# A spatially adaptive convolution in two layers: half of image 0's preparation moved from the prologue into the main loop, with x loads, row stores and squares of the prologue rearranged

## The chip, the cores and the metric

One core of a Trainium2 chip runs the whole program. The metric is the device time of one execution in microseconds; a kernel's time is the median of its runs. Engines are called PE (TensorE matmul), DVE (VectorE), ACT (ScalarE), POOL (GpSimd) and SP (SyncE, which here only issues DMAs). Each engine works through its own queue of instructions in order.

## The reference, cut to what matters

The input x has 4 images of 16 channels, 256 x 256 pixels. Two layers follow; each normalises its input by groups of two channels (8 groups per image) and adds its result to it.

```
# layer 0: h = groupnorm(x); 25 logits per channel and pixel from a 3x3 convolution of h
logits  = conv3x3(h, conv_w) + conv_b              # 16 * 25 = 400 channels
weights = softmax(logits over the 25)
x = x + sum over the 25 of weights * (5x5 neighbourhood of h)
# layer 1: a 3x3 convolution of silu(h) and of 8 cubic B-spline bases of h, h = groupnorm(x)
x = x + conv3x3(silu(h), base_w) + conv3x3(bsplines(h), spl_w) + bias
```

## The kernel before, in words

The program has three stages. The prologue (from line 404 on) computes the group statistics of x, all four images, and prepares image 0. layer0 (line 620) is the main loop of layer 0. layer1 (line 886 on) does layer 1. Only the first two are touched.

**What "preparing" an image is.** Layer 0 reads its normalised input h from DRAM in three layouts: hs (rows, cut in strips, with borders of two pixels; it gives the 5x5 neighbourhoods, tile u), hst (columns, f32; it gives the convolution's main operand, tile am) and hsl (columns again, split into a rounded part hi and a remainder lo; it gives tile an). The columns of hst and hsl are kept apart for the upper and the lower 128 rows of the image (half 0 and half 1), each with one row of the other half as its border. normalize (line 264) is a generator that makes them, for four groups of four channels (q) and both halves (h):

- rows(q): for each half, ACT writes the row tile hsp (line 327) and the column-ordered tile ht (line 340), two instructions each; put_rows (line 286) stores hsp to hs.
- columns(q, n, h): PE transposes four blocks of ht into the PSUM tile tp (line 362); tt and hi are copied from it with the border row (lines 355 to 359), hi always by ACT, tt by DVE in the prologue and by ACT in the main loop; DVE computes lo = tp - hi (line 370); border (line 312) copies lo's border rows. put_columns (line 294) stores tt, hi and lo, a DMA each for each half (line 302): 16 calls of columns and 48 such DMAs per image.

A step of the generator ends at each yield. Stores and loads are put into a list, moves, with the number of steps after which they are issued. All of them are on SP's queue.

**The prologue.** x comes in 8 tiles of 128 rows (four images, two halves; line 423). The first two stay in SBUF (held), the others rotate through three buffers (xin, bufs=3). For each tile, DVE takes bn_stats for every group (lines 534 and 536), with two steps of image 0's normalize after each group; then ACT squares the tile (xq, line 543, one instruction) and PE sums the squares over channels (line 546), from which a bound on the logits is made. At the end of each image come group_stats (small operations, line 140 on), and after all of it a flag (line 589) that says whether the softmax may leave out its maximum. SP loads that flag (line 1112), every engine branches on it, and layer0 starts. A tile scheduler, not the program text, fixes the order on each engine in this stage.

**The main loop.** Each image is worked in 16 strips of 128 rows by 32 columns (two halves of 8 strips), each strip in 8 steps of 4 columns: PE makes logits lg from am and an (lines 833, 837), ACT takes the exponential e (line 856), POOL multiplies by the neighbourhood (line 861), DVE sums over the 25 (nd, line 700) one step later. Three DVE operations and a POOL operation finish a strip (lines 720 to 728); every four strips ACT does the statistics for layer 1 (line 748) and stores the result. load_im (line 640) fetches am and an two pairs of steps ahead, load_u (line 667) a strip's u half a strip ahead, all on SP. In every step one step of the next image's normalize is taken (ahead): images 1 to 3 are prepared in the loop of the image before. The order here is pinned to the text. e has 4 buffers, am and an 3, lg 3, tp 1.

Throughout, every DMA issue on SP or ACT also takes one of 8 completion counters in turn and waits until that counter's DMA before it has landed.

Of the kernel before, what the change touches and what calls it, by code (L numbers as in the profile page):

```python
# [34 lines left out]
def conv_preact_kernel(  # L35
# [34 lines left out]
    QC = 4  # L70
# [192 lines left out]

    def normalize(b, ptr, tiles, held=None, copier=None):

# [4 lines left out]

        moves = [(20 + 4 * i, f) for i, f in enumerate(zeros(b, nc.sync))] if held is None else []

        def move():
            for f in [f for i, f in moves if i <= 0]:
                f()
            moves[:] = [(i - 1, f) for i, f in moves if i > 0]

        def load(q, h):
            if held is None and q < C // QC:
                nc.sync.dma_start(  # L280
                    xps[h][:, :, PAD : PAD + W],
                    x[b, q * QC : (q + 1) * QC, h * P : (h + 1) * P, :].rearrange(
                        "c p w -> p c w"),
                )

        def put_rows(q, h, hsp):
            r0 = PAD + h * P
            nc.sync.dma_start(
                hs[b][:, r0 : r0 + P, q * QC : (q + 1) * QC, :].rearrange(
                    "s r c w -> r s (c w)"),  # L290
                hsp.rearrange("p s c w -> p s (c w)"),
            )

        def put_columns(q, n):
            g0 = n * QG
            for h in range(NH):

# [19 lines left out]
        def rows(q):  # L317
            for h in range(NH):
                xp = xps[h] if held is None else held[h][:, q * QC : (q + 1) * QC]
                hsp = prep.tile([P, NST, QC, SP], F32, name=f"hsp{b}_{q}_{h}", tag="hsp")  # L320
                ht = prep.tile([P, QW, W // QW, QC], F32, name=f"ht{b}_{q}_{h}", tag=f"ht{h}")
                hts[q, h] = ht
                for k in range(QC // GC):
                    g = q * (QC // GC) + k
                    kc = slice(k * GC, (k + 1) * GC)
                    how = dict(scale=nrm[b][:, 0, g : g + 1], bias=nrm[b][:, 1, g : g + 1])
                    nc.scalar.activation(
                        hsp[:, :, kc, :].rearrange("p s c w -> p c s w"),
                        bass.AP(
                            tensor=xp.tensor, offset=xp.offset + k * GC * (W + 2 * PAD),  # L330
                            ap=[xp.ap[0], [W + 2 * PAD, GC], [SW, NST], [1, SP]],
                        ),
                        AF.Identity, **how,
                    )
                    if k == QC // GC - 1:
                        nc.scalar.copy(hsp[:, 0, :, 0:PAD], zpad)
                        nc.scalar.copy(hsp[:, NST - 1, :, PAD + SW :], zpad)
                        moves.append((4, partial(put_rows, q, h, hsp)))
                    yield
                    nc.scalar.activation(  # L340
                        ht[:, :, :, kc].rearrange("p g w c -> p c w g"),
                        xp[:, kc, PAD : PAD + W].rearrange("p c (w g) -> p c w g", g=QW),
                        AF.Identity, **how,
                    )
                    if k == QC // GC - 1:
                        moves.append((4, partial(load, q + 1, h)))
                    yield

        def columns(q, n, h):

            tp = ptr.tile([P, QG, P], F32, name=f"tp{b}_{q}_{n}_{h}", tag="tp")

            def copy(t, to):

                to(t[:, h, :, 1 : 1 + P], tp)
                if h == 0:
                    to(t[:, 1, :, 0:1], tp[:, :, P - 1 :])
                else:
                    to(t[:, 0, :, RP - 1 :], tp[:, :, 0:1])

            for k in range(QG):
                nc.tensor.transpose(
                    tp[:, k, :], hts[q, h][:, n * QG + k].rearrange("p w c -> p (w c)"), ident
                )
            yield
            copy(tts[n], copier)
            copy(his[n], nc.scalar.copy)
            yield

            nc.vector.tensor_sub(  # L370
                los[n][:, h, :, 1 : 1 + P], tp, his[n][:, h, :, 1 : 1 + P].bitcast(F32)
            )
            if h == NH - 1:
                moves.append((5, partial(border, los[n])))
                moves.append((9, partial(put_columns, q, n)))
            yield
# [3 lines left out]

        for h in range(NH):
            load(0, h)
        yield
        for _ in rows(0):
            move()
            yield
        for q in range(C // QC):
            ahead = rows(q + 1) if q + 1 < C // QC else iter(())
            for n in range(QW // QG):
                for h in range(NH):  # L390
                    for k, _ in enumerate(columns(q, n, h)):
                        if k % 3 == 2:
                            next(ahead, None)
                        move()
                        yield
# [8 lines left out]
    with tc.tile_pool(name="prep0", bufs=2) as prep, tc.tile_pool(  # L404
        name="pre", bufs=1
    ) as pre, tc.tile_pool(
        name="xin", bufs=3
    ) as xin, tc.tile_pool(name="stat", bufs=2) as stat, tc.tile_pool(
# [33 lines left out]
        for r in (4 * C, 6 * C):  # L442
            nc.sync.dma_start(wnr[r : r + 1, :], conv_b)
        nm = 3 * C
        sw = pre.tile([P, 3, 9, nm], F32, name="sw")
# [50 lines left out]
        def prepare1():  # L496
# [10 lines left out]
            for r in range(RT):  # L507
# [3 lines left out]
                for d in range(3):  # L511
                    p = SROWS.index(r + d) * C
                    nc.sync.dma_start(
                        ws[p : p + C, :, r, :],
                        wb1[d * C : (d + 1) * C].rearrange("p (e o) -> p e o", e=3),
                    )
# [4 lines left out]
        hm = pre.tile([P, B * NH], F32, name="hm")  # L521
        xq = pre.tile([P, C, W], F32R, name="xq")
        idr = pre.tile([P, P], F32R, name="idr")
        nc.scalar.copy(idr, ident)
        ahead = iter(())
        for b in range(B):
            st = stat.tile([P, G, NH * (GC if b == 0 else 1), 6], F32, name=f"st0_{b}", tag=f"st0{min(b, 1)}")
            for hf in range(NH):
                n = b * NH + hf
                t = loaded.pop(0)  # L530
                for g in range(G):
                    if b == 0:
# [8 lines left out]
                    next(ahead, None)  # L541

                nc.scalar.activation(xq, t, AF.Square)
                sq = pstat.tile([P, W], F32, name=f"sq_{n}", tag="sq")
                for c in range(C):
                    nc.tensor.matmul(
                        sq, lhsT=idr, rhs=xq[:, c], start=c == 0, stop=c == C - 1
                    )
                nc.vector.tensor_reduce(hm[:, n : n + 1], sq, AX.X, ALU.max)
                next(ahead, None)  # L550
                if n >= NH and n + 3 < B * NH:
                    loaded.append(load_x(n + 3))
            mean, rstd = group_stats(stat, pstat, st, f"x{b}")
# [19 lines left out]
            if b == 0:  # L573
                ahead = normalize(0, ptr0, tiles, held, nc.vector.tensor_copy)
                next(ahead)
# [44 lines left out]
    def layer0(shift):  # L620
# [4 lines left out]
        with tc.tile_pool(name=f"prep{arm}", bufs=2) as prep, tc.tile_pool(  # L625
# [172 lines left out]
            for n, (b, hf, s) in enumerate(strips):  # L798
                if (hf, s) == (0, 0):
                    for _ in ahead:  # L800
                        pass
                    ahead = normalize(b + 1, ptr, tiles) if b + 1 < B else iter(())
                    if b == B - 1:
# [3 lines left out]
                if last:  # L807
                    for _ in ahead:
                        pass
                u = us.pop(0)  # L810
# [351 lines left out]
```

## Time and profile before

| what | us |
|---|---|
| median of 3 runs | 3069.55 |
| lowest and highest of them | 3064.12, 3075.65 |
| the profiled execution, its own time | 3061.86 |
| its span, first to last instruction | 3059.8 |
| DVE busy in the span | 2959.0 (97%) |
| PE busy | 2802.6 (92%) |
| ACT busy | 2236.6 (73%) |
| POOL busy | 1947.6 (64%) |
| first nd (line 700) starts | 136.9 |
| last nd | 2043.9 |

The three stages show in the span like this: the prologue until about 120 us, layer 0 until about 2064 us, layer 1 until the end. DVE's reductions (512 of them, 1748.0 us together) and POOL's products (512, 1788.4 us) fill layer 0. An idle time in these views is put down to what released the engine; where several things were waited for, it is the last.

### The profile page before, as it was taken

How to read it: one execution, taken by the hardware profiler on the slowest of the kernel's cores; microseconds unless marked ns; L12 is line 12 of the kernel's file. 1: busy time of each engine (PE TensorE's matmuls, PEld its weight loads, DVE VectorE, ACT ScalarE, POOL GpSimd, SP SyncE). 2: the span in 40 equal slices, each digit the busy share in tenths (PEclk: the TensorE clock that was granted, in tenths of full speed). 3: DMA queues.
4: the chain of work that ended last, by engine and by line, in shares of the span. 5: the costliest groups of instructions: out<-in, count | busy, mean ns of one | idle time of the engine just before them, and what ended most of it. 6: DMA issues, size and time to landing. Idle time of an engine off the chain costs nothing.

```text
span 3059.8 us, 39743 instructions
## 1 busy us (share of the span) xinstructions
PE 2802.6 (92%) x14248; PEld 1448.2 (47%) x14248; DVE 2959.0 (97%) x1587; ACT 2236.6 (73%) x2587; POOL 1947.6 (64%) x744
## 2 busy tenths in 40 slices
PE   4499999999999999999999999958999999999998
PEld 3366656656656666666666566632222222222222
DVE  7599999999999999999999999998999999999997
ACT  6466765676766566766646546559999999999996
POOL 4199999999999999999999999980100100000000
PEclk7699999999999999999999999978999999999999
DMA  8988977879878778978767667659999999999994
GB/s 273 290 223 221 258 205 209 222 189 257 234 209 240 196 202 225 248 216 220 212 174 200 164 173 194 161 131 198 201 192 195 198 194 189 198 194 202 190 197 91
DMA packets 350929, 626.29 MB, mean 205 GB/s; under 512 B 41330, under 2 KB 216676, under 8 KB 334852
## 3 DMA queue, kind: packets, MB, share of 16 engines
q1 hardware_dynamic: 318020, 605.29, 81.0%
q10 hardware_dynamic: 30960, 15.73, 1.8%
q0 software_dynamic: 1744, 2.64, 0.3%
q8 instruction: 117, 1.92, 0.3%
q14 instruction: 88, 0.72, 0.1%
HBM read 513.95 MB, written 104.24 MB: 202 GB/s over the span
## 4 chain that ended last, share of the span: by engine, by line
DVE 69%; issue 11%; PE 8%; DMA 3%; ACT 3%; POOL 2%; SPq 1%; DVEq 0%; ACTq 0%; POOLq 0%
DVE nd L700 44%; PE lg L833 6%; DVE ta L168 4%; DVE ta L167 4%; DVE tb L168 4%; DVE tb L167 4%; DVE tb L158 2%; PE lg L837 1%; DVE yo L1020 1%; POOL e L861 1%; DVE r L721 1%; DVE nd L720 1%; DVE lo L370 1%; DMA am<-hst 1%; DVE nd L722 1%
## 5 line engine op out<-in xcount | busy, mean ns | idle before, releaser
L861 POOL TENSOR_TENSOR e<-e,u 128x1600 f32<-128x1600 f32 x512 | 1788.4, 3539 | 49.0 <-ACT e L856 30.9
L833 PE MATMUL lg<-wm,am 128*128 128x400 f32 x4096 | 1734.8, 505 | 83.8 <-ACT e L856 53.0
L700 DVE TENSOR_REDUCE nd<-e 128x128 f32<-128x3200 f32 x512 | 1748.0, 3478 | 29.0 <-POOL e L861 28.9
L837 PE MATMUL lg<-wn,an 97*128 97x400 f32 x2048 | 1344.9, 657 | 17.3 <-DMA an<-hsl 17.3
L856 ACT ACTIVATE e<-lg 128x800 f32<-128x800 f32 x1024 | 818.2, 837 | 708.9 <-DVE nd L700 460.5
L833 PEld LDWEIGHTS lg<-wm,am 128*128 128x128 f32 x4096 | 760.9, 192 | 403.3 <-ACT e L856 98.2
L1037 PE MATMUL yp<-ring,wt 128*32 128x512 f32 x6144 | 745.9, 598 | 87.6 <-DVE ring L169 63.7
L837 PEld LDWEIGHTS lg<-wn,an 97*128 97x128 f32 x2048 | 388.3, 190 | 334.5 <-issue 23.6
L1037 PEld LDWEIGHTS yp<-ring,wt 128*32 128x32 f32 x6144 | 203.7, 109 | 621.7 <-issue 427.7
L954 POOL MEMSET sl<- 16x256 f32 x6 | 1.8, 306 | 402.7 <-ACT ta L163 299.8
L169 DVE SCALAR_TENSOR_TENSOR ring<-ta,ta 128x2048 f32<-128x2048 f32 (+1 forms) x64 | 147.9, 2310 | 2.5
L168 DVE TENSOR_TENSOR ta<-ta,ta 128x2048 f32<-128x2048 f32 (+1 forms) x64 | 147.5, 2305 | 2.8 <-ACT ta L166 2.8
L169 DVE SCALAR_TENSOR_TENSOR ring<-tb,tb 128x2048 f32<-128x2048 f32 x64 | 145.6, 2275 | 2.5
L748 ACT ACTIVATE z<-xc,nrm 128x256 f32<-128x256 f32 x240 | 144.2, 601 | 5.3 <-POOL xc L728 1.2
L168 DVE TENSOR_TENSOR tb<-tb,tb 128x2048 f32<-128x2048 f32 x64 | 145.4, 2271 | 0.0
L1047 PE MATMUL yp<-sl,ws 64*32 64x512 f32 (+1 forms) x1032 | 131.3, 602 | 0.0
L954 POOL MEMSET slc<- 16x256 f32 x2 | 0.6, 307 | 203.1 <-ACT ta L163 203.0
L166 ACT ACTIVATE ta<-ta 128x2048 f32<-128x2048 f32 (+1 forms) x64 | 123.4, 1928 | 2.0
L193 POOL TENSOR_TENSOR d<-d,nrz 128x8 f32<-128x8 f32 x4 | 2.7, 669 | 191.8 <-DVE d L191 191.8
L166 ACT ACTIVATE tb<-tb 128x2048 f32<-128x2048 f32 x64 | 120.6, 1884 | 0.0
L973 ACT ACTIVATE sl<-sl,q 64x2048 f32<-64x2048 f32 x43 | 90.0, 2094 | 1.1
L728 POOL TENSOR_TENSOR xc<-xc,nd 128x512 f32<-128x512 f32 x64 | 82.5, 1289 | 8.2 <-DVE nd L722 8.2
(195 smaller groups left out, 2089.3 us busy)
## 6 DMA issues: line engine op xcount, KB each, us to landing
am<-hst SPq DMA_DIRECT2D x512, 194.6 KB
u<-hs SPq DMA_DIRECT2D x320, 288.0 KB
an<-hsl SPq DMA_DIRECT2D x512, 129.8 KB
xta<-x1s SPq DMA_DIRECT2D x40, 1024.0 KB
xtb<-x1s SPq DMA_DIRECT2D x40, 1024.0 KB
xtc<-x1s SPq DMA_DIRECT2D x40, 1024.0 KB
am<-hst SPq DMA_DIRECT2D x256, 129.8 KB
sl<-x1s SPq DMA_DIRECT2D x166, 128.0 KB
```

Of the source, the lines that this page charges most:

```text
L166: nc.scalar.activation(s1, r1, AF.Square, scale=2.0)
L167: nc.vector.scalar_tensor_tensor(s2, t, 2.0, s2, ALU.subtract, ALU.mult)
L168: nc.vector.tensor_mul(s1, s1, r1)
L169: nc.vector.scalar_tensor_tensor(f, s2, 0.0, s1, ALU.min, ALU.subtract if given else ALU.add)
L700: nc.vector.tensor_reduce(nd[:, :, :, j : j + JG].rearrange("p t c j -> p t j c"), e.rearrange("p t j m c d -> p t j c m d"), AX.XY, ALU.add,)
L748: nc.scalar.activation(z, v, f, scale=nrm[b][:, 0, g : g + 1], bias=nrm[b][:, 1, g : g + 1], accum_out=st1[b][:, t, g, columns_of(n) : col ...
L833: nc.tensor.matmul(lg[:, i, :NL], lhsT=am[:, o : o + P], rhs=wm.rearrange("p m c d -> p (m c d)"), start=True, stop=False,)
L837: nc.tensor.matmul(lg[:, i, :NL], lhsT=an[:, o : o + P], rhs=wn.rearrange("p m c d -> p (m c d)"), start=False, stop=True,)
L856: nc.scalar.activation(ev, lg[:, :, :NL], AF.Exp)
L861: nc.gpsimd.tensor_tensor(e[:, 1].rearrange("p j m c d -> p j (m c) d"), e[:, 0].rearrange("p j m c d -> p j (m c) d"), uv, ALU.mult,)
L1037: nc.tensor.matmul(yp[t * M : (t + 1) * M], lhsT=wt[:, d, e].rearrange("p r o -> p (r o)"), rhs=ring[:, r0 + t * RT + d : r0 + t * RT + d ...
L1047: nc.tensor.matmul(yp[t * M : (t + 1) * M], lhsT=ws[v, e].rearrange("p r o -> p (r o)"), rhs=sl[n % 3][v, t : t + NT + 1 : NT, e : e + W], ...
```

## The change: what it does

Of image 0, the prologue makes columns only for half 0. normalize gets an argument part.

- **part=0**, in the prologue: rows are done as before for both halves, and all transposes too, but from half 1 only one border row is copied; of tt, hi and lo a full tile is made for half 0 alone. The border rows that half 1 will need from half 0 are put aside in new constant tiles (kept). put_columns stores half 0 only: 24 DMAs.
- **part=1** (late), in the main loop during image 0's first strips: x's half 1 is loaded again (4 loads of 512 KB), ht is made again, columns are made for half 1 and stored (24 DMAs). tt is copied by ACT here. It must be through before strip 6, and after it follows the preparation of image 1, as a chain.
- **dense=True** for late and for image 1: columns takes 4 steps instead of 6, transposes, copies and lo within one of them.
- **Loads of x**: xin has 4 buffers instead of 3, and tile 5 is loaded right after the convolution's weights.
- **put_rows** in the prologue is issued on ACT's queue, after 1 step instead of 4.
- **Squares**: xq is made in two halves (two buffers), with the PE sums, and stands ahead of the tile's bn_stats in the program.
- The six small DMAs to ws (line 513) go from SP's to POOL's queue.

```diff
-    def normalize(b, ptr, tiles, held=None, copier=None):
+    NQ = QW // QG
+    kept = [
+        const.tile([P, C // QC * NQ, QG, 1], d, name=f"kept{i}") for i, d in enumerate((F32, F32R, F32R))
+    ]
+    def normalize(b, ptr, tiles, held=None, copier=None, part=None, dense=False):
...
+        moves = moves if held is None and part is None else []
+        parts = range(NH) if part is None else (part,)
+        read = range(NH) if part != 1 else (1,)
...
+        def place(q, h):
+            return xps[h if part is None else q % 2]
...
-            nc.sync.dma_start(
+            (nc.sync if held is None else nc.scalar).dma_start(
                 hs[b][:, r0 : r0 + P, q * QC : (q + 1) * QC, :].rearrange(
...
-            for h in range(NH):
+            for h in parts:
                 for to, ti, t in ((hst, 0, tts[n]), (hsl, 0, his[n]), (hsl, 1, los[n])):
...
-                        moves.append((4, partial(put_rows, q, h, hsp)))
-                    yield
+                            moves.append((4 if held is None else 1, partial(put_rows, q, h, hsp)))
+                        yield
...
-            def copy(t, to):
-                to(t[:, h, :, 1 : 1 + P], tp)
-                if h == 0:
-                    to(t[:, 1, :, 0:1], tp[:, :, P - 1 :])
+            def copy(t, to, keep):
+                if h in parts:
+                    to(t[:, h, :, 1 : 1 + P], tp)
+                if part == 1:
+                    to(t[:, 1, :, 0:1], keep[:, q * NQ + n])
+                elif h == 1:
+                    to(t[:, 0, :, RP - 1 :], tp[:, :, 0:1])
                 else:
-                    to(t[:, 0, :, RP - 1 :], tp[:, :, 0:1])
+                    to(t[:, 1, :, 0:1] if part is None else keep[:, q * NQ + n], tp[:, :, P - 1 :])
...
-            yield
-            copy(tts[n], copier)
-            copy(his[n], nc.scalar.copy)
-            yield
+            if not dense:
+                yield
+            copy(tts[n], copier, kept[0])
+            copy(his[n], nc.scalar.copy, kept[1])
+            if not dense:
+                yield
+            v = slice(1, 1 + P) if h in parts else slice(RP - 1, RP)
+            to = h if h in parts else 0
             nc.vector.tensor_sub(
-                los[n][:, h, :, 1 : 1 + P], tp, his[n][:, h, :, 1 : 1 + P].bitcast(F32)
+                los[n][:, to, :, v], tp[:, :, 0 : v.stop - v.start],
+                his[n][:, to, :, v].bitcast(F32),
             )
+            if part == 0 and h == 0:
+                moves.append((1, partial(
+                    nc.scalar.copy, kept[2][:, q * NQ + n], los[n][:, 0, :, P : P + 1]
+                )))
+            if part == 1:
+                nc.scalar.copy(los[n][:, 1, :, 0:1], kept[2][:, q * NQ + n])
             if h == NH - 1:
-                moves.append((5, partial(border, los[n])))
-                moves.append((9, partial(put_columns, q, n)))
+                if part is None:
+                    moves.append((5, partial(border, los[n])))
+                moves.append((9 if part is None else 4, partial(put_columns, q, n)))
...
-        name="xin", bufs=3
+        name="xin", bufs=4
...
+        loaded.append(load_x(5))
...
-                    nc.sync.dma_start(
+                    nc.gpsimd.dma_start(
                         ws[p : p + C, :, r, :],
...
+                sq = pstat.tile([P, W], F32, name=f"sq_{n}", tag="sq")
+                for i in range(2):
+                    xq = pre.tile([P, C // 2, W], F32R, name=f"xq_{n}_{i}", tag="xq", bufs=2)
+                    nc.scalar.activation(xq, t[:, i * C // 2 : (i + 1) * C // 2], AF.Square)
+                    for c in range(C // 2):
+                        nc.tensor.matmul(
+                            sq, lhsT=idr, rhs=xq[:, c], start=i + c == 0,
+                            stop=(i, c) == (1, C // 2 - 1),
+                        )
                 for g in range(G):
...
-                nc.scalar.activation(xq, t, AF.Square)
-                sq = pstat.tile([P, W], F32, name=f"sq_{n}", tag="sq")
-                for c in range(C):
-                    nc.tensor.matmul(
-                        sq, lhsT=idr, rhs=xq[:, c], start=c == 0, stop=c == C - 1
-                    )
...
-                if n >= NH and n + 3 < B * NH:
-                    loaded.append(load_x(n + 3))
+                if n >= NH and n + 4 < B * NH:
+                    loaded.append(load_x(n + 4))
...
-                ahead = normalize(0, ptr0, tiles, held, nc.vector.tensor_copy)
+                ahead = normalize(0, ptr0, tiles, held, nc.vector.tensor_copy, 0)
...
-                    ahead = normalize(b + 1, ptr, tiles) if b + 1 < B else iter(())
+                    ahead = normalize(b + 1, ptr, tiles, dense=b == 0) if b + 1 < B else iter(())
+                    if b == 0:
+                        late = normalize(0, ptr, tiles, part=1, dense=True)
+                        ahead = chain(late, ahead)
...
+                if n == NST - 2:
+                    for _ in late:
+                        pass
```

## The prediction

> **What bounds the kernel now.** I read the busy time per stretch first, then DVE's and ACT's own timelines around the start of layer 0, then the waits.
>
> Stretches of 20 us (columns: length; busy us and instructions of PE, PE's weight load, DVE, ACT, POOL; granted clock; DMA share; GB/s), and below them a stretch of the main loop from another answer of the same view:
>
> ```profile
> 80.00:100.00 20.00, 11.45 (x52) 10.17 (x53) 14.46 (x31) 16.12 (x23) 0.00 (x0) 0.59 1.05 339
> 100.00:120.00 20.00, 6.13 (x32) 4.78 (x31) 14.63 (x52) 7.14 (x22) 1.84 (x2) 0.59 1.07 359
> 120.00:140.00 20.00, 13.47 (x40) 8.27 (x41) 3.09 (x1) 3.35 (x4) 7.24 (x18) 0.76 1.01 253
> 140.00:160.00 20.00, 12.09 (x35) 7.43 (x34) 10.34 (x4) 9.62 (x13) 9.91 (x4) 0.74 0.78 190
> ...
> 660.00:1170.00 510.00, 484.12 (x1693) 312.02 (x1691) 508.26 (x206) 337.62 (x598) 493.83 (x153) 0.98 0.81 218
> ```
>
> From 660 to 1170 us DVE is busy 508.26 of 510: layer 0 is DVE's. So the change can save only before DVE's dense run begins, and each DVE instruction that it puts into the loop is paid in full. The dense run begins here:
>
> ```profile
> 136.91 6.97 DVE L700 TENSOR_REDUCE nd<-e 128x128 f32<-128x3200 f32 x2 [16.95 <-POOL e L861]
> 153.11 3.49 DVE L700 TENSOR_REDUCE nd<-e 128x128 f32<-128x3200 f32 x1 [9.23 <-POOL e L861]
> 157.03 3.49 DVE L700 TENSOR_REDUCE nd<-e 128x128 f32<-128x3200 f32 x1 [0.43 <-POOL e L861]
> 161.04 24.49 DVE L700 TENSOR_REDUCE nd<-e 128x128 f32<-128x3200 f32 x7 [0.53 <-POOL e L861]
> ```
>
> Two sums, a hole of 9.2 us, then no idle worth naming. The hole is ACT's (its timeline):
>
> ```profile
> 135.04 0.84 ACT L856 ACTIVATE e<-lg 128x800 f32<-128x800 f32 x1 [0.87 <-PE lg L837]
> 147.17 0.87 ACT L327 ACTIVATE hsp<-xp,nrm 128x576 f32<-128x576 f32 x1 [11.30 <-DMA am<-hst]
> 147.94 1.54 ACT L856 ACTIVATE e<-lg 128x800 f32<-128x800 f32 x2
> ```
>
> ACT stands at the first hsp of image 1 until its x has landed, and the third e is behind it. Before that, from the chain in order of time, the branch and the first load of the loop:
>
> ```profile
> 119.00 0.89 SPq L1112
> 120.44 0.60 SPq L648
> ```
>
> Call the start of that first am load T0 = 120.44. Its sequel does not depend on when it comes: u has landed at T0+12.9 (POOL's first product, 133.35), the first nd is at T0+16.5, image 1's x at T0+26.7. SP's waits say what holds the prologue back (us in total, times, longest):
>
> ```profile
> SPq L288 <- ACT hsp L337: 13.9, 2, 13.7
> SPq L288 <- DMA xin<-in_x_dram: 3.5, 1, 3.5
> SPq L302 <- DVE tt L355: 3.4, 4, 1.7
> ```
>
> SP stands at row stores until ACT has made the rows; the x loads are queued behind. The last x tile is issued only at 84.7 and its statistics start at 95.2.
>
> **The change, part by part.** The times are those of the profiled execution (3061.86 us; span 3059.8); the median of the three runs is 3069.55, 7.7 us more, and I carry the difference over.
>
> *Loads.* With four xin buffers tile 5 needs no release, and row stores no longer stand ahead of tiles 6 and 7. In the new order on SP, tile 5 and 6 follow the bias of the convolution, which waits for tile 4 (landed about 41, where the DMA engines run dry) and for the first row store: both are issued at about 44 and landed by 60 (a tile takes some 8 us: tile 1 landed 7.7 us after tile 0). Tile 7 is behind image 0's first six column stores, about 67, landed 76. No statistics wait for x any more; the prologue becomes a matter of ACT and DVE.
>
> *ACT in the prologue.* From 35.3 (first hsp) to 116.2 (its last instruction) ACT is busy 63.3 us. Off: 8 full hi copies (588 ns) -4.7, and 16 border copies of lo (200 ns) become 8: -1.6. On: the row stores, 8 issues x 382 ns (the median of the same stores on SP) +3.1; the squares, 5 tiles in two pieces. For that no row has the size; 128x2048 ACTIVATEs of layer 1 take 2079 ns and 128x4096 ones 3805, so two pieces cost 353 ns more, less about 0.12 of overlap between neighbours: +1.2. Bounds: 0 (PE starts half a tile earlier) to 1.8. Sum 61.3, so ACT cannot end before 96.6.
> On top come its waits. I walked the new ACT, DVE and PE queues side by side with the measured spacings (hsp+ht 1.84, bn_stats 0.61, hi 0.48, lo 0.60, xq 3.62). ACT waits 1.7 us for whi, since POOL now issues the six ws DMAs (0.5 us each) ahead of its weight copies; 1.4 for DVE's wn; and at three copies of lo's border into kept, which sit in ACT's queue ahead of DVE's lo, 2.5, 2.0 and 1.2. Behind each stand rows and squares. Together 8.8: ACT ends at 105.4.
>
> *DVE in the prologue.* 64.7 us in the same stretch, less 8 tt copies (0.68) and 8 lo (0.69), with 8 and 8 tiny ones (0.15) instead: about 56, so it could end at 92. ACT ends later and sets the end.
>
> *The flag.* It hangs on the last squares, about 1 us before ACT's end: 104.4, then PE's second half 1.9, hm and its scaling 0.9, and as before 2.2 from the maximum (111.21) to the flag (113.4), then 1.44 from SP's load of it to the am load: T0 = 110.9. Column stores used to stand ahead of that flag load (it waited from 113.4 to 119.0 for its turn); now 24 instead of 48, and the last are issued by 108, so this wait goes and ACT's end is what is late next. A walk by spacings leaves out handoffs; I add 2 us: T0 = 112.9, 7.5 us earlier.
>
> One rule of the Trainium skill speaks against the row stores on ACT ("DMA: Bandwidth & Descriptors", section Issuing engines are not separate DMA queues): issuing from several engines saves only the sequencer's time for the issue. By it the move hands 3.1 us from SP, which has time, to ACT, which has none: a loss of 3. The rows above say that SP lost 13.9 us at those stores, not by issuing but by standing in order, and it is the x loads behind them that this frees. I keep both: the loads gain, and ACT pays its 3.1.
>
> *The hole after T0.* late loads two tiles at its first step, takes an idle step, and starts its first ht one step later than image 1's hsp came before. So three e, not two, pass ahead of the wait. The x lands at T0+26.7 as before (same loads ahead of it on SP). Then ht 1.1 instead of hsp 0.77; nd follows 0.3 later, at T0+33.0, and before it DVE has three sums (3 x 3.40): the hole is 33.0 - 16.5 - 10.2 = 6.3 instead of 9.2. Gain 2.9. Bounds: 0 (a later x) to 9.2 (none).
>
> *The main loop.* 8 full lo more on DVE, 0.60 each from start to start (681 ns mean in the loop): +4.8, with no cover. ACT gets about 25 us over late's strips (8 ht 1.32, 8 tt 0.58, 8 hi 0.62, borders); its busy share there is two thirds, so this is hidden, except where the statistics for layer 1 fall (16 x (0.60 + 0.19) us in a strip): before, such a strip has ACT work of about 31.4 us against DVE's 29.6, with image 1 dense 33.5. POOL already stands 3.5 to 5 us there (300-330, 660-690) and DVE does not, since up to two e lie ready. For three such strips I take 0.5 each: +1.3 with rounding up; bounds 0 to 6. PE: transposes of 0.44 us, two sets a strip, against 2 us of its spare time a strip; nothing. SP: 6.4 MB of stores and 2.1 MB of loads move here, 1.7 MB a strip against the 4.8 that a strip loads; 286 GB/s occurred (210-240) with no idle DVE; nothing, bounds 0 to 25 (rival below).
>
> Sum: -7.5 - 2.9 + 4.8 + 1.3 = -4.3, so 3057.6 in the profiled execution, 3065 on the median's scale.
>
> **The rivals.** 0.5% (15 us) is about what a measurement of this kernel can tell from no change.
>
> A, the sum above: 3065, within 0.5%. For it: DVE's 508 of 510, which takes back two thirds of what the prologue gives. Chance 0.52.
>
> B, the prologue doesn't get shorter: the DMA engines are 93% busy from 35 to 116 us, and if they set the pace, or the kept copies cost ACT more than walked, T0 stays. Then -2.9 + 4.8 + 1.3 = +3: 3073. Against it: 24 stores of 0.27 MB, 6.4 MB of the stretch's 24 (301 GB/s x 81 us), are gone. Chance 0.23.
>
> C, much more goes: ACT hardly waits (T0 = 105, -15) and the hole closes (-9): -24 + 5 = -19: 3050. For it: the floors are those of the queues' own work. Against: both at once. Chance 0.17.
>
> D, slower: late's column stores on SP. Each set of three waits for DVE's lo, and the next am load is queued behind it; PE runs up to four steps ahead of DVE, so SP may come to the store a step (3.7 us) too early. If PE has no lead left, in strips 0 to 5, each of the 8 sets costs a step: 8 x 3.7 = 30, less the rest: 3069.55 - 4 + 30 = 3095. It decides once loads land less than a step ahead of their matmuls; before, PE waited for an four times in 150 to 660, 4.3 us in all, and DVE never. Chance 0.08.
>
> **How the numbers follow.** A and B lie within 0.5%: 0.52 + 0.23 = 0.75. C is faster, 0.17; D slower, 0.08. The range takes A and B with the unknown costs, and C to its value: 3049 to 3079.
>
> **What would show it.** Right: the flag load between 110 and 115; ACT, not SP or DMA, ahead of it; a hole of about 6 us after three nd; 56 full lo in the loop and no new idle on DVE until 660. Wrong: T0 at 105 or at 120; holes of DVE at late's stores, released through am; POOL short of e in the strips with statistics, with DVE idle behind it.

## The result, and the profile after

| | before | after |
|---|---|---|
| median, runs side by side on the same chip (us) | 3064.06 (7 runs) | 3053.29 (7 runs) |
| lowest and highest | 3061.24, 3075.65 | 3048.49, 3054.58 |
| profiled execution, its span | 3061.86, 3059.8 | 3048.49, 3046.7 |
| T0, the first am load of layer 0 | 120.44 | 110.62 |
| first nd starts | 136.91 | 125.78 |
| DVE idle from the first nd until its dense run | 10.2 | 4.1 |
| DVE busy from 170 to 600 us (430 us) | 428.97 | 428.97 |
| last DVE operation of layer 0 starts (lines 722, 764) | 2063.12 | 2050.84 |
| from there to the end of the span | 996.7 | 995.9 |

The ratio after to before is 0.9956, with a 95% interval of 0.994 to 0.9972: the kernel is faster, by 0.28 to 0.60%. It is the ratio of the means; the medians give 0.9965. Three of the seven runs before are those of the table further up (3064 to 3076 us), while beside the experiments the kernel before had medians of 3061.2 to 3061.7, against which 3053.29 is about 0.9973. So the gain of the total is 8 to 13 us: around the 0.5% that the forecast drew as its bound, and two to three times the 4.3 us that it took as likeliest. Lines moved: nd is now line 742, am 690, lo 397.

Stretches of the kernel after, with the columns of those shown of before:

```profile
80.00:100.00 20.00, 12.20 (x57) 11.12 (x58) 10.07 (x42) 19.51 (x32) 1.84 (x2) 0.59 0.53 184
100.00:120.00 20.00, 9.61 (x37) 7.10 (x36) 7.28 (x20) 6.16 (x10) 0.59 (x16) 0.61 0.71 230
120.00:140.00 20.00, 17.66 (x57) 10.91 (x57) 10.47 (x3) 9.77 (x13) 13.98 (x4) 0.91 1.07 252
140.00:160.00 20.00, 20.00 (x74) 13.26 (x73) 19.63 (x8) 13.76 (x23) 19.17 (x7) 1.00 0.94 243
660.00:1170.00 510.00, 483.54 (x1691) 312.59 (x1691) 507.38 (x205) 335.41 (x589) 494.35 (x154) 0.98 0.82 220
```

From 80 to 100 us ACT is busy 19.51 of 20 (before 16.12), and the DMA share has fallen from 1.05 to 0.53: in this stretch ACT sets the pace, as forecast. From 140 on DVE is dense (19.63 of 20; before 10.34). The stretch from 660 to 1170 is as it was.

DVE's timeline where its dense run begins (start, length, engine and line, operation, and in brackets the idle time before it and what ended it):

```profile
125.78 6.98 DVE L742 TENSOR_REDUCE nd<-e 128x128 f32<-128x3200 f32 x2 [12.27 <-POOL e L910]
133.13 3.49 DVE L742 TENSOR_REDUCE nd<-e 128x128 f32<-128x3200 f32 x1 [0.38 <-POOL e L910]
140.10 3.49 DVE L742 TENSOR_REDUCE nd<-e 128x128 f32<-128x3200 f32 x1 [3.48 <-POOL e L910]
143.50 0.68 DVE L397 TENSOR_TENSOR lo<-tp,hi 128x512 fp32r<-128x512 f32 x1
144.10 3.48 DVE L742 TENSOR_REDUCE nd<-e 128x128 f32<-128x3200 f32 x1
147.85 10.46 DVE L742 TENSOR_REDUCE nd<-e 128x128 f32<-128x3200 f32 x3 [0.27 <-POOL e L910]
```

Three sums pass before the hole, which is 3.48 us. The first lo of late, 0.68 us, stands among the sums with nothing to cover it. ACT's timeline has the hole's cause:

```profile
128.65 0.84 ACT L905 ACTIVATE e<-lg 128x800 f32<-128x800 f32 x1 [0.88 <-PE lg L886]
133.81 1.29 ACT L360 ACTIVATE ht<-xp,nrm 128x512 f32<-128x512 f32 x1 [4.32 <-DMA xp<-in_x_dram]
134.90 1.57 ACT L905 ACTIVATE e<-lg 128x800 f32<-128x800 f32 x2
```

ACT still stands at work for a later strip until x has landed, but x lands at T0 + 23.2 now (133.81 - 110.62), not at T0 + 26.7.

The account by position: the first nd comes 11.1 earlier (9.8 of it T0), the idle time behind it is 6.1 shorter, eight more full lo cost 4.8: -12.4. The last DVE operation of layer 0 comes 12.3 earlier. So in these two profiles nothing was lost or won on balance in the rest of the loop.

### The profile page after: what moved, and what is told of

Its sections match the earlier page's. It is cut to its first block, busy times and chain, and to the rows that moved or that the text cites. A ratio compares the mean times of both kernels' runs of the same rounds, so it can differ in the third digit from the quotient of the medians.

```text
span 3046.7 us, 39869 instructions
## 1 busy us (share of the span) xinstructions
PE 2801.7 (92%) x14280; PEld 1448.9 (48%) x14280; DVE 2954.5 (97%) x1587; ACT 2251.5 (74%) x2627; POOL 1952.8 (64%) x750
## 4 chain that ended last, share of the span: by engine, by line
DVE 73%; issue 11%; DMA 5%; PE 5%; ACT 4%; POOL 1%; SPq 1%; DVEq 0%; POOLq 0%; ACTq 0%
DVE nd L742 49%; DVE ta L169 4%; DVE ta L168 4%; DVE tb L169 4%; DVE tb L168 4%; PE lg L882 3%; DVE tb L159 2%; DVE yo L1069 1%; DVE r L763 1%; DVE nd L762 1%; DVE lo L397 1%; DVE nd L764 1%; POOL e L910 1%; DMA xin<-in_x_dram 1%; PE yp L1086 1%
```

## The experiments

All are edits of the kernel after, timed against the kernel before. One reading has to come first. Layer 1, which no edit touches, took 995 us in some profiled executions and up to 1007 in others, so a span alone misleads. T0, the first nd and the last DVE operation of layer 0 are read from one profile each, and the total by the ratio over all runs.

| kernel | runs | ratio, 95% interval | median us | T0 | first nd | idle behind it | last DVE op of layer 0 |
|---|---|---|---|---|---|---|---|
| after | 7 | 0.9956 (0.994 to 0.9972) | 3053.29 | 110.62 | 125.78 | 4.1 | 2050.84 |
| no_split | 11 | 0.9985 (0.9976 to 0.9995) | 3057.82 | 114.60 | 130.60 | 5.9 | 2053.76 |
| split_only | 20 | 0.9967 (0.9958 to 0.9977) | 3051.28 | 108.83 | 125.67 | 4.2 | 2055.67 |
| rows_on_sp | 4 | 0.9949 (0.9932 to 0.9966) | 3048.07 | 105.11 | 122.30 | 5.2 | 2050.71 |
| xin_three | 20 | 0.9977 (0.997 to 0.9984) | 3053.42 | 111.64 | 126.83 | 4.4 | 2054.69 |
| lo_twice | 13 | 0.9978 (0.9968 to 0.9988) | 3057.74 | 110.10 | 126.79 | 4.0 | 2059.85 |
| kept_pool | 6 | 0.9959 (0.9944 to 0.9973) | 3051.6 | 107.18 | 123.97 | 4.5 | 2052.52 |
| step_later | 6 | 0.9952 (0.9939 to 0.9966) | 3051.99 | 110.14 | 126.37 | 1.3 | 2052.93 |
| squares_whole | 12 | 0.9996 (0.9982 to 1.001) | 3060.01 | 118.08 | 134.16 | 3.7 | 2063.10 |
| squares_rows | 8 | 0.9957 (0.9945 to 0.9969) | 3047.54 | 107.13 | 122.54 | 4.5 | 2048.20 |
| squares_one_ahead | 20 | 0.9978 (0.9968 to 0.9988) | 3055.42 | 112.10 | 129.43 | 5.1 | 2057.38 |
| rows_step | 6 | 0.9951 (0.9934 to 0.9968) | 3048.26 | 104.81 | 121.25 | 0 | 2044.67 |
| rows_step_kept | 6 | 0.9938 (0.9922 to 0.9955) | 3043.04 | 103.61 | 120.35 | 2.4 | 2050.69 |

The ratio compares each kernel with the kernel before of its own session: beside the twelve variants that had medians of 3061.2 to 3061.7, beside the kernel after 3064.06. So the 0.9956 of the kernel after is not on quite the same footing as the ratios below it, and where a total is compared with it, the medians are given too.

My theory: half 1's columns are work taken off the prologue, ACT's end falls with it, and DVE pays eight lo for it. The rivals: the gain is the earlier x loads, or the DMA engines' load, or the squares.

**The two halves of the change.** no_split keeps the loads, the row stores on ACT and the squares, and prepares all of image 0 in the prologue; split_only does the reverse.

```diff
# no_split
-                ahead = normalize(0, ptr0, tiles, held, nc.vector.tensor_copy, 0)
+                ahead = normalize(0, ptr0, tiles, held, nc.vector.tensor_copy)
...
-                    ahead = normalize(b + 1, ptr, tiles, dense=b == 0) if b + 1 < B else iter(())
-                    if b == 0:
-                        late = normalize(0, ptr, tiles, part=1, dense=True)
-                        ahead = chain(late, ahead)
+                    ahead = normalize(b + 1, ptr, tiles) if b + 1 < B else iter(())
```

```diff
# split_only
-            (nc.sync if held is None else nc.scalar).dma_start(
+            nc.sync.dma_start(
...
-        name="xin", bufs=4
+        name="xin", bufs=3
...
-                for i in range(2):
-                    xq = pre.tile([P, C // 2, W], F32R, name=f"xq_{n}_{i}", tag="xq", bufs=2)
...
+                nc.scalar.activation(xq, t, AF.Square)
```

> The changed kernel with image 0 prepared whole in the prologue again (no part, no late, image 1 not dense); loads, row stores on ACT, squares and ws stay as changed. Time before 3064, after 3053. Theory of the record (ACT's and DVE's own queues set the prologue's end, the split shortens both, and the loop pays 4.8): T0 about 117 instead of 110.6, hole about 9 instead of 4, 8 full lo fewer in the loop: 3053 + 6 + 5 - 5 = 3059. Rival loads (all of the prologue's gain is the freed x loads): T0 stays at 111, so 3053 + 5 - 5 = 3053. Rival DMA (the 24 stores are what counted): T0 about 120, 3063.

> The kernel before with the split of image 0 alone (part, late, dense); three xin buffers, row stores and ws on SP, squares whole and behind the statistics as before. Theory of the record: x tiles 6 and 7 still come late behind row stores, T0 about 117, hole 4 to 6, lo +4.8: about 3060. Rival loads: T0 stays at 120, 3063. Rival DMA: T0 111, 3053.

no_split has 0.9985 and T0 = 114.6, between my theory's 117 and the 111 of the rival loads. split_only has 0.9967 and T0 = 108.8: my theory's 117 missed by 8, and the 111 of the DMA rival was nearer. I had let the x loads come as late as before, but the last x tile was issued at 76.8 instead of 84.7, with nothing done to the loads themselves. The split is the larger part, and the rest is worth something by itself. But the parts do not add at T0: with the split alone layer 0 starts 1.8 us earlier than with the whole change, and by the medians (3051.28 and 3053.29) the whole change is not faster than the split alone. Something in the rest costs the prologue time once the split is there.

The hole is shorter without the split too, 5.9 us, against 10.2 before: the x of the next image lands at T0 + 22.7 in no_split, at T0 + 26.7 before.

The DMA rival says that T0 follows the load on the DMA engines. In the stretch from 35.3 to 116.2 us the two kernels had 263 GB/s (split_only) and 323 (no_split), against 301 before, so no_split came earlier than before with more traffic. And in these three kernels neither DVE nor ACT waits for an x load between 35 and 116 us. So that rival falls as what sets T0.

**Which of the rest.** rows_on_sp gives the row stores back to SP's queue, xin_three takes away the fourth buffer with its load orders, squares_whole puts the squares back whole and behind the statistics.

```diff
# rows_on_sp
-            (nc.sync if held is None else nc.scalar).dma_start(
+            nc.sync.dma_start(
...
-                            moves.append((4 if held is None else 1, partial(put_rows, q, h, hsp)))
+                            moves.append((4, partial(put_rows, q, h, hsp)))
```

```diff
# xin_three
-        name="xin", bufs=4
+        name="xin", bufs=3
...
-        loaded.append(load_x(5))
...
-                if n >= NH and n + 4 < B * NH:
-                    loaded.append(load_x(n + 4))
+                if n >= NH and n + 3 < B * NH:
+                    loaded.append(load_x(n + 3))
```

> The changed kernel with image 0's row stores on SP's queue again, after 4 steps; all else as changed. Theory of the record: SP stands at the stores, loads and column stores behind them are late, T0 3 to 5 later than 110.6: 3056 to 3058. Rival[...]: ACT gets its 8 x 0.4 us back, T0 up to 3 earlier: 3050 to 3053.

> The changed kernel with three xin buffers, tile 5 not loaded early, as before; all else as changed. Theory of the record: ACT sets the pace and x lands with some 10 us to spare, so one tile less ahead costs little: T0 up to 2 later, 3053 to 3055. Rival loads: the fourth buffer is the gain, T0 5 or more later, 3058 and up.

> The changed kernel with the squares in one piece and behind the statistics, as before. Theory of the record: ten pieces cost about 1 us more than five whole ones, but the flag hangs on the last squares: whole ones add half a tile's matmuls (1.9 us) behind ACT's end, and the order on the engines shifts: T0 0 to +3, 3053 to 3056. Rival (the order ahead of the statistics is the gain): T0 5 or more later, 3058.

rows_on_sp: T0 falls to 105.1. My theory had it 3 to 5 us later than 110.6, the rival up to 3 earlier, so the direction is the rival's and the size neither's. The last x tile is still issued at 67.5 (66.3 in the kernel after), so the early loads do not need the stores on ACT. xin_three: the last x tile is issued at 72.9, 6.6 later, and T0 moves by 1.0 only, within the 0 to 2 of my theory. The rival of the loads falls at T0. The totals are not told apart: the ratio is worse, the medians are equal (3053.42 and 3053.29). In the profile the first nd comes 1.05 later and the last DVE operation 3.9; the rest is small DVE waits in the loop, 3.4 us in all between 170 and 1040 against 1.5.

squares_whole: T0 = 118.1, nearly all of the gain gone. My theory (0 to 3 later) missed, the rival (5 or more) came. DVE's timeline of squares_whole at the end of the prologue:

```profile
113.67 0.42 DVE L589 TENSOR_REDUCE hm<-sq 128x1 f32<-128x256 f32 x1 [7.12 <-PE sq L586]
...
116.34 0.14 DVE L629 CAST flag<-bd 1x1 int32<-1x1 f32 x1
```

DVE stands 7.12 us for the last squares, which ACT made only at 106.18. The same place in rows_on_sp:

```profile
93.87 0.41 DVE L591 TENSOR_REDUCE hm<-sq 128x1 f32<-128x256 f32 x1
...
99.14 0.17 DVE L596 COPY nrm<-rstd_x 128x8 f32<-128x8 f32 x1 [1.75 <-POOL rstd_x L155]
...
102.84 0.13 DVE L631 CAST flag<-bd 1x1 int32<-1x1 f32 x1
```

Here the maximum hm is taken at 93.87 without a wait, and the flag hangs on the last tile's statistics. In the kernel after it is the reverse: the last statistics begin at 79.8, the last squares on ACT at 102.46. Two chains lead to the flag. With the row stores on ACT, the squares are the late one; on SP, the statistics are.

**Where the squares stand.** Two more kernels separate this. squares_rows is squares_whole with the row stores on SP. squares_one_ahead keeps the stores on ACT and the squares ahead of the statistics, but makes them in one piece.

```diff
# squares_one_ahead
-                for i in range(2):
-                    xq = pre.tile([P, C // 2, W], F32R, name=f"xq_{n}_{i}", tag="xq", bufs=2)
-                    nc.scalar.activation(xq, t[:, i * C // 2 : (i + 1) * C // 2], AF.Square)
...
+                xq = pre.tile([P, C, W], F32R, name=f"xq_{n}", tag="xq", bufs=1)
+                nc.scalar.activation(xq, t, AF.Square)
```

> Row stores back on SP, and the squares whole and behind the tile's statistics as before; four x buffers stay. With the stores on ACT this form of the squares had T0 at 118.1 (last squares on ACT at 106.2). Theory: the store's place in ACT's and SP's order is what pushes the squares behind the columns, so without it T0 is 106 to 109, near the 108.8 of the split alone. Rival one: the two edits are independent and add (105.1 + 7.5): T0 112 to 113. Rival two: the squares' form alone sets the end: T0 117 to 118.

> Row stores on ACT as in the change, squares in one piece with one buffer, but ahead of the tile's statistics in the program. Theory: the place in the program decides (the squares behind the statistics came 7.5 us late), not the pieces: T0 110 to 113. Rival: the pieces decide, through the second buffer, which lets ACT go on while PE still reads the first: T0 116 to 118.

squares_rows has T0 = 107.1: inside the theory's 106 to 109, and neither the sum (112 to 113) nor the squares' form alone (117 to 118). Put behind the statistics and made whole, the squares cost 7.5 us at T0 with the stores on ACT and 2.0 with the stores on SP. The two edits interact, and the order on ACT shows how: the last squares end at 109.8 in squares_whole and at 91.2 in squares_rows, at 104.4 in the kernel after and at 89.1 in rows_on_sp. Why the scheduler lays them so, no run here shows. squares_one_ahead has T0 = 112.1, inside the theory's 110 to 113. Of the 7.5, the place in the program is 6.0 (118.08 - 112.10), the pieces with their second buffer 1.5. Its ratio, 0.9978, is worse than 1.5 us explain; the first nd came 17.3 us after its T0 instead of 15.2, and the rest is spread over the loop.

**The copies into kept.** I had put 5.7 us of ACT's waits on them. kept_pool makes them on POOL.

```diff
# kept_pool
-                    nc.scalar.copy, kept[2][:, q * NQ + n], los[n][:, 0, :, P : P + 1]
+                    nc.gpsimd.tensor_copy, kept[2][:, q * NQ + n], los[n][:, 0, :, P : P + 1]
```

> The changed kernel with the 8 copies of lo's border into kept made by POOL instead of ACT. ACT waited 6.9 us at them in its queue. Theory of the record (ACT's queue sets T0): T0 4 to 6 earlier, about 105.5, 3048. Rival (DVE's queue or the last x tile is right behind): T0 at most 1 to 2 earlier, 3052.

T0 falls by 3.4 (107.18), between the theory's 4 to 6 and the rival's 1 to 2, the first nd by 1.8, and the total not measurably (0.9959). The waits were on the path; not all of what they gave arrives. ACT's last instruction of the prologue ends 5.8 us earlier (100.1 instead of 105.9), but DVE then stands 2.4 us for PE's last sums of squares instead of 0.7.

**The hole.** step_later starts late's first ht one step later.

```diff
# step_later
         if part == 1:
             yield
+            yield
         for _ in rows(0):
```

> The changed kernel with one more idle step of late before its first ht, so that four e pass ahead of the wait for x. T0 unchanged. Theory of the record (the hole is ACT standing in order at x): the hole of 4.1 us closes, -3.5: 3049.5. Rival (the hole is PE or POOL filling up again after the start): it stays, 3053.

The idle time behind the first nd goes from 4.1 to 1.3, as the theory has it, though x landed later there (T0 + 25.1). The total, 0.9952, is not told apart from 0.9956: small DVE waits of 5.0 us between 170 and 1040 (4.7 of them for POOL) stand where the kernel after has 1.5.

**What a lo costs.** lo_twice computes each full lo of late twice, with the same values.

```diff
# lo_twice
-            nc.vector.tensor_sub(
+            for _ in range(2 if part == 1 else 1):
+              nc.vector.tensor_sub(
...
```

> The changed kernel with the 8 full lo of late computed twice (the same values again). Theory of the record: DVE has no slack in the loop, each full lo costs 0.60: +4.8 on 3053, 3058, and the last nd 4.8 later against the first. Rival (slack behind POOL hides it): no difference, 3053.

DVE's timeline of lo_twice at the first pair:

```profile
144.62 1.41 DVE L398 TENSOR_TENSOR lo<-tp,hi 128x512 fp32r<-128x512 f32 x2
145.95 13.65 DVE L743 TENSOR_REDUCE nd<-e 128x128 f32<-128x3200 f32 x4
```

The next sum starts 1.33 us after the pair, where it starts 0.60 after a single lo in the kernel after (143.50 to 144.10). So a second lo costs 0.73, eight of them 5.8, and no slack hides them. The last DVE operation of layer 0 comes 9.0 us later: 1.0 of it is the first nd, 5.8 the eight lo, and 2.2 small waits between 170 and 1040 (3.7 instead of 1.5). The total agrees in size (medians 3057.74 and 3053.29, 4.5 us; ratios 0.0022 apart, 6.7 us), but the intervals of the two ratios overlap slightly.

**The best pieces together.** rows_step has the row stores on SP and late one step later. rows_step_kept has the copies on POOL too.

> Row stores of the prologue back on SP and late one step later, together. Alone, the first brought T0 from 110.6 to 105.1, the second the hole from 4.1 to 1.3 us. Theory: both are time ahead of DVE's dense run and add up: T0 near 105, hole below 2, the first kernel that gains clearly more than the change itself: ratio 0.9935 to 0.9945 (3043 to 3046 us). Rival: DVE's small waits between 170 and 1040 us (1.5 us in the changed kernel, 4.7 with the later step) take it back: ratio 0.995 or more.

> The same, and the copies of lo's border into kept made by POOL instead of ACT. Theory: with the rows on SP the last squares are done by 91 and the flag no longer hangs on ACT, so taking ACT's waits away gives nothing more: T0 104 to 105.5, ratio as of the kernel without it, within 0.0007. Rival: ACT's waits are still what is late: T0 falls by the 3.4 us that they were worth in the changed kernel, to about 102, ratio 0.0011 lower.

For rows_step the theory holds for T0 (104.8) and the hole, but the ratio, 0.9951, is the rival's: the small waits of DVE are 3.5 us between 170 and 1040. DVE's timeline where the dense run begins:

```profile
121.25 17.45 DVE L743 TENSOR_REDUCE nd<-e 128x128 f32<-128x3200 f32 x5 [13.83 <-POOL e L911]
138.62 0.68 DVE L397 TENSOR_TENSOR lo<-tp,hi 128x512 fp32r<-128x512 f32 x1
139.22 13.67 DVE L743 TENSOR_REDUCE nd<-e 128x128 f32<-128x3200 f32 x4
```

Five sums and then the first lo, with no hole. ACT waits 0.46 us for x:

```profile
127.06 0.84 ACT L906 ACTIVATE e<-lg 128x800 f32<-128x800 f32 x1 [0.87 <-PE lg L887]
128.37 1.34 ACT L360 ACTIVATE ht<-xp,nrm 128x512 f32<-128x512 f32 x1 [0.46 <-DMA xp<-in_x_dram]
```

In this profile the last DVE operation of layer 0 comes at 2044.67, 18.5 us earlier than before and 6.2 earlier than in the kernel after. The total does not show it: its six runs lie at 3039.8 to 3046.5 and at 3050.0 to 3052.1, three each. rows_step_kept has the lowest ratio of all, 0.9938, but its T0, 103.6, is only 1.2 us earlier than that of rows_step and fits neither the theory (104 to 105.5) nor the rival (about 102), and in its one profile layer 0 ended 6 us later. Both beat the kernel before. Whether either beats the kernel after is not settled: the intervals overlap.

## Why the prediction was right, and where its sizes were off

**What bounds the kernel: right.** Layer 0 is DVE's, gains come only ahead of its dense run, and a lo in the loop is paid in full (lo_twice).

**T0: right mechanism, a term too much, and some luck.** The walk of the queues gave ACT's end at 105.4 and T0 at 110.9; measured were 105.9 and 110.62. The 2 us that I added for handoffs were not there. The flag's chain is as I had it; DVE's timeline of the kernel after:

```profile
106.43 0.42 DVE L591 TENSOR_REDUCE hm<-sq 128x1 f32<-128x256 f32 x1 [0.66 <-PE sq L576]
...
108.89 0.14 DVE L631 CAST flag<-bd 1x1 int32<-1x1 f32 x1
```

and SP's, where the last column store goes out 2 us before the flag, so the wait for it is gone:

```profile
106.36 0.57 SPq L320 DMA_DIRECT2D hsl<-lo  x1
110.62 1.86 SPq L690 DMA_DIRECT2D am<-hst  x3
```

This wait is the larger part of the gain at T0: before, 7.2 us lay between the flag and the first am load (113.25 to 120.44), after, 1.7 (108.89 to 110.62). Of the 9.8, 5.5 are that, and 4.4 the earlier flag.

Inside the sum two terms were off and cancelled. ACT's waits of the kernel after between 35 and 115 us (total, times, longest):

```profile
ACT kept L288 <- DVE lo L397: 6.9, 5, 2.4
...
ACT hsp L347 <- DMA hs<-hsp: 2.5, 2, 2.0
ACT wn L520 <- DVE wn L519: 1.5, 1, 1.5
...
ACT whi L518 <- POOL wp L516: 0.6, 1, 0.6
```

I had 5.7 at kept, 1.4 at wn, 1.7 at whi. I had not foreseen the 2.5 us that ACT stands for its own row stores to leave hsp, nor 1.0 at hi. In all ACT is idle for 12.7 us between its first hsp and its end, where I had 8.8. Against that stand the row stores: I had 3.1 us of ACT's time for their issues, and the trace has next to none. ACT's computing takes 58.4 us until its end, where the forecast has 58.2 without the issues; with the 12.7 of idle time that fills the stretch. From ACT's timeline (ACTq is an issue):

```profile
66.94 1.91 ACT L574 ACTIVATE xq<-xin 128x2048 fp32r<-128x2048 f32 x1
67.06 0.37 ACTq L306 DMA_DIRECT2D hs<-hsp  x1
68.75 0.56 ACT L376 CAST hi<-tp 128x512 fp32r<-128x512 f32 x1
```

The issue lies inside a piece of squares that is already running, and the next instruction starts 1.81 us after that piece, as it does after the next piece, which has no issue inside (69.27 to 71.08). All eight issues lie so inside a running instruction; inside the short hi copies they delay the next instruction by 0.1 us at most (0.53 to 0.57 from start to start, elsewhere 0.47 to 0.53). That the walk met ACT's end so closely is therefore luck in part.

**From T0 to the first nd: not unchanged.** I held it at 16.5. It was 15.2, since u landed at T0 + 11.6 (POOL's first product, 122.23). Over the kernels it lies between 15.2 and 17.3. After T0 = 105.1 in rows_on_sp it was 17.2, which gives back 2.0 of the 5.5 that T0 won there.

**The hole: right in kind, half in size.** Three sums do pass ahead of it. "The x lands at T0+26.7 as before" failed: it landed at T0 + 23.2. Of these 3.5 us the first nd, itself 1.3 nearer to T0, takes 1.3 back; with small differences in the sums and the short waits around the hole the gain is 6.1 instead of 2.9. Why x lands sooner after T0, no run here settles; over the kernels it ranges from 22.7 to 26.7. That the extra idle step is what closes the hole is shown by step_later.

**The main loop: +4.8 held, +1.3 was not there in this profile.** DVE is busy 428.97 us of 430 between 170 and 600 both before and after. The answer for after:

```profile
170.00:600.00 430.00, 414.70 (x1476) 269.64 (x1475) 428.97 (x182) 292.45 (x513) 418.06 (x130) 0.99 0.86 240
```

ACT's 292.45 there is 15.8 more than before (276.68), and hidden. But one profile does not refute the +1.3. In that stretch DVE has no waits in the two kernels without late (before, no_split) and none in the kernel after, while in each of the other eleven kernels with late it waits for POOL, 0.4 to 4.7 us in all. These waits fall during layer 1's statistics on ACT or within some 8 us behind them, which is where I had put the +1.3 and one of the signs of being wrong that I had named. ACT's extra work is not shown to be their only cause: at the third statistics PE also stood for am, 3.4 to 4.6 us in kept_pool, split_only and squares_whole.

Put together: 2.3 at T0, 1.3 behind it, 3.2 in the hole, 1.3 in the loop, 8.1 in all, is what lies between -4.3 and -12.4. All four errors point the same way, so the gain came out between A's 4.3 and C's 19. That the time still fell inside A's half per cent is partly luck: the interval, 0.28 to 0.60%, reaches over it.

**The row stores: wrong.** "The loads gain, and ACT pays its 3.1": the loads gain through the fourth buffer and tile 5's place, without the stores on ACT (rows_on_sp), and the gain of loads is small (xin_three, 1.0 at T0). The rule of the Trainium skill that I set against the rows ("DMA: Bandwidth & Descriptors", section Issuing engines are not separate DMA queues) says that issuing from several engines saves only the sequencer's time; from it I had read a loss of about 3. The measured loss is 5.5 at T0 and 3.5 at the first nd, but not by issue time, which cost ACT next to nothing (above). ACT's busy time is nearly the same in both kernels (58.4 and 58.0 us); its idle time is 2.4 larger in the kernel after, about the 2.5 that it waits for its stores to leave hsp, a wait that rows_on_sp does not have. The rest is the order: with the stores on ACT the last squares end at 104.4, with them on SP at 89.1. rows_on_sp moves the queue and the step (4 instead of 1) together, so which of the two reorders ACT is open. And I read SP's 13.9 us of standing at row stores as a cost of the path. In rows_on_sp SP stands 16.7 us there (10.9 for hsp, 5.8 for hi) and T0 is the earlier one; and before, neither DVE nor ACT waited for an x load between 35 and 116 us.

**The squares: mis-sized in what mattered.** I priced their two pieces at +1.2, from ACTIVATEs of layer 1. Two pieces take 3.70 us and a whole one 3.62, so five tiles cost 0.4. What I did not price was their place ahead of the statistics, worth 6.0 at T0 in this order of tasks. The walk had it without my naming it, since I walked the new queues.

**The rivals.** B (T0 stays) fell: 0.71 of DMA share from 100 to 120 us, and T0 moved by 9.8. C in full (T0 = 105, no hole) did not come with this change, but rows_step reaches it: T0 = 104.8, no hole, and 18.5 us at the end of layer 0 where C had 19. D (DVE stalls at late's stores, some 30 us) fell: DVE's waits between 170 and 600 add up to nothing in the kernel after and to 4.7 at most in the variants.

**Open.** Why the small DVE waits in layer 0 differ so between kernels with the same loop: between 170 and 1040 they are 0 (no_split) and 0.5 us (before) without late, and from 1.5 (after) to 5.0 (step_later) with it. Nearly all are releases by POOL, some behind ACT's e and some behind am or u, and one profile a kernel cannot say what is the kernel's and what the execution's.

## What to carry to other kernels

When a shared prologue feeds a loop that one engine bounds, find the two or three chains that lead to the start of the loop and walk each engine's new queue instruction by instruction with measured spacings. Here such a walk needed no margin on top, and it showed which chain was late next; check its terms one by one all the same, since two of them can be off and cancel. Judge a DMA issue moved to another queue by which engine ends the stage and by what the move does to the order there, not by how long the old queue stood or by the time of the issue: here SP stood 16.7 us at the row stores with T0 at 105.1, and with the issues on ACT, where they took next to none of its time, T0 was 5.5 later. Judge small edits by positions in the trace (T0, first and last operation of the stage) and by many runs, since an untouched stage differed by 10 us and more between two executions here.

## What the hardware showed that I had not expected

Layer 1 is the same code in all fourteen kernels and took 995.3 (squares_one_ahead) to 1007.1 us (squares_whole) from the last DVE operation of layer 0 to the end. Most of the difference between the two kernels shown here arises in its first 400 us. Kernel after (995.9 in all), then kept_pool (1005.8), from 2060 to 2460 us:

```profile
2060.00:2460.00 400.00, 372.24 (x3062) 93.50 (x3054) 391.43 (x217) 391.42 (x184) 22.43 (x22) 0.99 0.97 199
```

```profile
2060.00:2460.00 400.00, 368.07 (x2986) 93.60 (x2982) 383.31 (x212) 381.67 (x180) 22.80 (x23) 0.97 1.00 192
```

DVE and ACT are busy 8 to 10 us less in the second, at a DMA share of 1.00 instead of 0.97 and fewer GB/s (192 instead of 199): there the DMA engines were occupied longer for less. What makes one execution do so and another not, no run here shows.
